# Cross-attention on one core: low parts, a score tile, bias additions and normalization moved within the slots

## The chip, the cores and the metric

The kernel runs on one core of a Trainium2 chip. The metric is the device time of the core in microseconds (us). Five engines work beside each other, each through its own list of instructions in the order in which the program wrote them: TensorE (PE; its weight loads are listed apart as PEld), VectorE (DVE), ScalarE (ACT), GpSimd (POOL) and SyncE (SP). SP computes nothing here. It issues nearly all DMAs, also in order, and an issue whose data is not ready holds up those behind it.

## The reference

Thirty-two batch entries share one set of weights. Each has 512 query rows of width 640 and 77 text keys of width 1024. Only the text part of the context is present (77 rows), so the three other attentions of the original network have no keys and add nothing.

```python
q   = heads(x @ to_q_w)                 # 32 x 20 heads x 512 x 32
k   = heads(ctx @ to_k_w)               # 32 x 20 heads x 77 x 32
v   = heads(ctx @ to_v_w)
p   = softmax(q @ k.T / sqrt(32))       # over the 77 keys
out = merge(p @ v) @ to_out_w + to_out_b + x
```

Everything is float32. The kernel gets products of that quality out of a faster, reduced format: each operand is split into a high part (a copy rounded to that format) and a low part (the operand less its high part), and each product is the sum of three: high by high, high by low, low by high.

## The kernel before

**Stages.** In the first part (the first score product starts at 262.2 us, and the last values follow beside the first slots) the keys and values of all batches are computed from the context, split into parts and written to scratch memory in HBM. After that comes attention, in *slots*. The width of 640 is cut into five chunks of 128, which are four heads each. Slot n = 5b + j works on batch b, chunk j, so a batch takes five slots and there are 160 of them. `end()` closes the pipeline behind the last.

**What one slot does.** `slot(n)` is the whole schedule: engines run their instructions in the order in which this function writes them, and nothing reorders them. The buffer counts (`bufs=`) set which earlier reader an instruction has to wait for. In one slot several chunks are in flight:

- `scores(n, t)`, t = 0 to 3: three score products (L478) of 128 query rows with the keys of four heads, into one of three PSUM tiles; VectorE takes the row maximum (L486). `exps(n, t)`: ScalarE's four exponentials with their sums (L496).
- `queries(n+1, ...)`: fifteen products (L443) for the next chunk's queries, then `split_q(n+1)`: ScalarE's high copy (L454), two GpSimd casts (L458) and two VectorE subtractions (L460). The next slot's scores need all of them.
- `sums(n-1)` takes the reciprocal of the sums (VectorE, L506), `normalize(n-1)` multiplies the probabilities of the last chunk by it (GpSimd, L511, one instruction of 16 rows of 77), and `transpose_p(n-1)` turns them in 32 by 32 blocks (VectorE, L518) and stores them to scratch memory (four DMAs, L525).
- `load_p(n-3)` fetches older probabilities back (L534, L535), now with keys along partitions. For the chunk `taken` = n-4, `cast_p` makes their high parts on ScalarE (L542 for the last 64 rows, L543 for the rest), `last_p` the low part of those 64 rows on GpSimd (L556) and `rest_p` that of the rest on VectorE (L549). All four write one buffer, `pp`.
- `values(taken)` is six value products (L570). The first two read L543's result; the third and fourth read rows written by L542 and L556 together; the fifth and sixth read L549's. They write `pa`, of which there is one. `sum_a` copies its upper half (ScalarE, L581) and adds it to the lower (VectorE, L583). In the next slot `high_a` and `low_a` split the sum (ScalarE L590, VectorE L595); this frees `pa`.
- `piece(batch, i)`: output products (L613), 24 per slot, of an earlier batch, in two pieces of 12 (6 and 18 in slot 4). `finish()` adds residual and bias to finished halves of an output tile (VectorE, L642) and sends the tile out (L648).

**Residual and bias.** An output tile has 128 rows; each batch has four, t = 0 to 3. `load_residual` (SP, L602) fetches rows of x into one of three buffers `xr`; `add_bias` (GpSimd, L606) adds the bias to them. Two tables say in which slot j of a batch b this happens, as (how many batches back, t): `RESIDUAL = {1: (1, 0), 3: (1, 1), 4: (1, 2), 0: (2, 3)}` and `BIAS = {2: (1, 0), 4: (1, 1), 0: (2, 2), 1: (2, 3)}`. So in a batch's slot 0, tile 3 of the batch before the last is fetched, and in slot 1 its bias is added. Tile 0 of the last batch is fetched in slot 1 and gets its bias in slot 2, where the first of its additions in `finish` is two slots away.

**Other work in the slots.** `split_x` (ScalarE L264, GpSimd L265) and `transpose_x` (VectorE L257) prepare the next batch's x; `copy_keys` (GpSimd, L423, L424) doubles some key rows, for one group of chunks in slot 1 and for the other in slot 4; `refill` and `load_x` fetch keys, values and x (L419, L432, L253).

**Orders that the change touches.** GpSimd's order in slot 1 is `copy_keys`, `last_p`, `normalize`, the two casts of `split_q`, `add_bias`; in slot 0 it is `last_p`, `normalize`, casts, `add_bias`. VectorE runs `rest_p` and then `low_a`, except in slot 4, where `low_a` is first. SP's order in slot 0 is: one fetch of x, four of keys, the two of `load_p`, four more of keys, the residual, and then the four stores of `transpose_p`.

## Time and profile before

| What | us |
|---|---|
| runs shown: median of 3 (lowest to highest) | 1933.45 (1927.69 to 1944.38) |
| the profiled execution: its own time | 1923.57 |
| its span, first to last instruction | 1921.7 |
| mean granted TensorE clock in it | 0.992 |
| GpSimd's bias additions, L606 | 128 of 1.584 each, 202.7 in all |
| GpSimd's normalization, L511 | 160 of 3.147 each, 503.5 in all |
| VectorE's low part of the probabilities, L549 | 160 of 1.632 each |
| VectorE's low part of attention, L595 | 160 of 0.680 each |

The profile is of one execution, which lies 0.5% under the median of the runs shown. Its times are from the start of the span. A row of a group gives the busy time, the mean of one instruction, and the idle time of the engine before these instructions with what ended it. Matmuls are pipelined and their ends are modelled, so TensorE's progress is better read from the starts of its instructions than from its busy time. In a timeline, a row can stand for several like instructions (x12), and the bracket at its end gives the idle time before it and the instruction or DMA that ended it.

### The profile page before, as it was taken

The page shows a single profiled execution, that of the slowest core. Times are in us where ns is not written, and L with a number is a line of the kernel's source. Part 1 is how long each engine was busy: PE and PEld are TensorE (multiplying, and loading weights), DVE is VectorE, ACT ScalarE, POOL GpSimd, SP SyncE. Part 2 cuts the span into 40 slices and gives each one's busy share as a digit, 9 for nine tenths or more (in the row PEclk, how much of TensorE's full clock was granted, in tenths as well). Part 3 has the DMA queues.
Part 4 walks back from the last instruction along what each step waited for, and adds up shares of the span by engine and source line. Part 5 has one row for each costly group of instructions (what it writes and reads, how often), then busy time and mean ns, then how long its engine had stood idle before and what let it go on. Part 6 is the DMA issues. An engine that isn't in the chain of part 4 may idle for free.

```text
span 1921.7 us, 37548 instructions
## 1 busy us (share of the span) xinstructions
PE 1883.1 (98%) x10332; PEld 1665.2 (87%) x10332; DVE 1626.7 (85%) x2494; ACT 1526.3 (79%) x6210; POOL 1422.3 (74%) x1116
## 2 busy tenths in 40 slices
PE   9999997999999999999999999999999999999998
PEld 7888886888888888888888889888888888888887
DVE  5444447899999989999999999999999999999985
ACT  3232247998998989899888899998998989999882
POOL 1100067888898888888888888888888888888873
PEclk9999998999999999999999999999999999999999
DMA  9878869898888888888989898898889888889875
GB/s 185 201 195 249 200 176 222 215 233 238 235 232 233 233 216 231 233 231 228 238 223 236 236 239 234 232 237 231 234 228 233 225 240 234 237 232 229 226 211 157
DMA packets 565022, 431.36 MB, mean 224 GB/s; under 512 B 191120, under 2 KB 473168, under 8 KB 564816
## 3 DMA queue, kind: packets, MB, share of 16 engines
q1 hardware_dynamic: 560304, 414.47, 84.0%
q0 software_dynamic: 4416, 14.34, 2.2%
q8 instruction: 85, 1.39, 0.3%
q14 instruction: 121, 0.99, 0.2%
q10 hardware_dynamic: 96, 0.16, 0.0%
HBM read 247.17 MB, written 181.64 MB: 223 GB/s over the span
## 4 chain that ended last, share of the span: by engine, by line
PE 44%; ACT 15%; DVE 14%; DMA 13%; issue 5%; SPq 5%; POOL 3%; DVEq 0%; POOLq 0%; ACTq 0%
PE pq L443 11%; PE po L613 11%; PE pv L191 6%; DMA raw<-pd 6%; ACT pn L496 6%; PE pk L191 6%; PE pa L570 5%; PE sc L478 4%; DVE pp L549 4%; DMA xs<-in_x_dram 3%; ACT pp L543 2%; DVE nm L486 2%; DVE z L518 2%; ACT xt L264 2%; ACT aw L581 2%
## 5 line engine op out<-in xcount | busy, mean ns | idle before, releaser
L496 ACT ACTIVATE pn<-sc,nm 128x77 f32<-128x77 f32 x2560 | 794.0, 333 | 32.6 <-DVE nm L486 27.7
L613 PE MATMUL po<-wo_s,at 128*128 128x320 f32 x3840 | 636.1, 314 | 7.3 <-DVE at L595 3.0
L443 PE MATMUL pq<-xt,wq_s 128*128 128x512 f32 x2400 | 621.4, 400 | 0.0
L613 PEld LDWEIGHTS po<-wo_s,at 128*128 128x128 f32 x3840 | 569.0, 189 | 15.9 <-DVE at L595 12.3
L496 ACT ACTIVATION_READ_ACCUMULATOR pn<-sc,nm 128x1 f32 x2560 | 545.7, 213 | 0.0
L511 POOL TENSOR_TENSOR pn<-pn,rs 128x1232 f32<-128x1232 f32 x160 | 503.5, 3147 | 23.8 <-DVE rs L506 12.3
L443 PEld LDWEIGHTS pq<-xt,wq_s 128*128 128x128 f32 x2400 | 429.9, 190 | 75.7
L478 PEld LDWEIGHTS sc<-kb,qt 128*128 128x128 f32 x1920 | 327.9, 189 | 59.7 <-POOL qt L458 12.1
L478 PE MATMUL sc<-kb,qt 128*128 128x154 f32 (+1 forms) x1920 | 317.9, 274 | 13.8 <-POOL qt L458 8.9
L486 DVE TENSOR_REDUCE nm<-sc 128x4 f32<-128x308 f32 x640 | 288.4, 451 | 44.1 <-PE sc L478 37.6
L549 DVE TENSOR_TENSOR pp<-raw,pp 128x1024 fp32r<-128x1024 f32 x160 | 261.1, 1632 | 31.0 <-ACT pp L543 24.9
L556 POOL TENSOR_TENSOR pp<-raw,pp 64x512 fp32r<-64x512 f32 x160 | 212.4, 1327 | 97.5 <-ACT pp L542 88.5
L570 PE MATMUL pa<-pp,vb 128*128 128x512 f32 x960 | 265.5, 407 | 10.0 <-DVE at L595 6.2
L518 DVE STREAM_TRANSPOSE z<-pn 128x1280 f32<-128x1280 f32 x160 | 241.9, 1512 | 8.0 <-DMA pd<-z 2.8
L583 DVE TENSOR_TENSOR pa<-pa,aw 64x512 f32<-64x512 f32 x320 | 222.7, 696 | 21.1 <-ACT aw L581 10.8
L460 DVE TENSOR_TENSOR qt<-pq,qt 64x512 fp32r<-64x512 f32 x320 | 219.2, 685 | 23.6 <-ACT qt L454 17.0
L265 POOL TENSOR_TENSOR xt<-xs,xt 128x512 fp32r<-128x512 f32 x160 | 202.6, 1292 | 34.0 <-ACT xt L264 30.7
L570 PEld LDWEIGHTS pa<-pp,vb 128*128 128x128 f32 x960 | 171.8, 190 | 57.8 <-DVE pp L549 13.2
L606 POOL TENSOR_TENSOR xr<-xr,bias 128x640 f32<-128x640 f32 x128 | 202.7, 1584 | 17.6 <-DMA xr<-in_x_dram 6.0
L458 POOL CAST qt<-qt 64x512 fp32r<-64x512 f32 x320 | 195.0, 609 | 21.7 <-ACT qt L454 2.0
L581 ACT COPY aw<-pa 64x1024 f32<-64x1024 f32 x160 | 161.9, 1012 | 47.5 <-PE pa L570 43.3
L542 ACT CAST pp<-raw 64x512 fp32r<-64x512 f32 x160 | 99.5, 622 | 97.6 <-DMA raw<-pd 97.3
(46 smaller groups left out, 1639.8 us busy)
## 6 DMA issues: line engine op xcount, KB each, us to landing
pd<-z SPq DMA_DIRECT2D x640, 160.0 KB, 3.5
raw<-pd SPq DMA_DIRECT2D x160, 512.0 KB, 4.0
xs<-in_x_dram SPq DMA_DIRECT2D x128, 320.0 KB, 7.2
xr<-in_x_dram SPq DMA_DIRECT2D x128, 320.0 KB, 3.8
out_dram<-xr SPq DMA_DIRECT2D x127, 320.0 KB, 3.7
raw<-pd SPq DMA_DIRECT2D x160, 128.0 KB, 4.2
v_dram<-vs SPq DMA_DIRECT2D x80, 192.0 KB, 4.1
k_dram<-ks POOLq DMA_DIRECT2D x20, 512.0 KB, 4.3
```

Source lines behind the costliest of these rows:

```text
L191: nc.tensor.matmul(held[j][:, :gn], w[:, k, a, :], cts[g, k][:, c, :gn], start=(k == 0 and n == 0), stop=(k == NK - 1 and n == 2),)
L443: nc.tensor.matmul(pqs[n], wq_s[:, k, a, j * P : (j + 1) * P], xts[b, k][:, c, :], start=(k == 0 and m == 0), stop=(k == NC_ - 1 and m == 2),)
L460: nc.vector.tensor_tensor(qt[r, 1 + w, :], pq[r], qt[r, 0, :].bitcast(F32), ALU.subtract)
L478: nc.tensor.matmul(sc[:, cols], qt[:, m, t * P : (t + 1) * P], keys_, start=(m == 0), stop=(m == 2),)
L486: nc.vector.tensor_reduce(nm, sc[:, :KCOLS].rearrange("p (h k) -> p h k", k=NKEY), AX.X, ALU.max, negate=True)
L496: nc.scalar.activation(pnb[n % 2][:, at, :NKEY], sc[:, i * NKEY : (i + 1) * NKEY], AF.Exp, bias=nm[:, i : i + 1], accum_out=sms[n][:, at : ...
L511: nc.gpsimd.tensor_tensor(pf, pf, rs.unsqueeze(2).to_broadcast([P, NQ * HPC, NKEY]), ALU.mult)
L518: nc.vector.transpose(z.rearrange("p b t j -> p t b j"), pn.rearrange("p (t h) k -> p t (h k)", t=NQ).rearrange("p t (b i) -> p t b i", i=Q),)
L549: nc.vector.tensor_tensor(pp[:, 2:4, :], raw[:, 0:2, :], pp[:, 0:2, :].bitcast(F32), ALU.subtract)
L570: nc.tensor.matmul(pas[n][:, p, :], vb[:, p, t, :], pp[:, c, :], start=(c == p), stop=(c == p + 2),)
L583: nc.vector.tensor_tensor(pa[64 * p : 64 * p + 64, 0], pa[:64, p], aw[:, p], ALU.add)
L613: nc.tensor.matmul(pos[b, t, h][:, :HALF], ats[b * NC_ + j][:, a, t * P : (t + 1) * P], wos[0][:, j, c, h * HALF : (h + 1) * HALF], start= ...
```

## The change

Seven things move; no arithmetic is added or left out.

1. `low_a` goes ahead of `rest_p` in slots 0 to 3. In slot 3, `high_a` also goes between the two casts of `cast_p`.
2. In slots 0 to 3, once output products run, the third score tile comes after four of the six value products instead of after all six.
3. The bias of tile 3 is added in slot 0 instead of slot 1, that of tile 0 in slot 1 instead of slot 2. The loads stay where they are.
4. `normalize` becomes two instructions of eight rows each. In slot 4 the second comes after the casts of `split_q`.
5. In slots 1 and 2 `normalize` goes ahead of `last_p`, and in slot 1 `copy_keys` goes from the slot's start to behind `last_p`.
6. In slots 4, 0 and 1 the reciprocal of the slot's own sums is taken at its end, ahead of the two additions of `sum_a`, instead of at the start of the next slot.
7. In slot 2 both splits of x come before the copy of `pa`, instead of one before and one after.

```diff
@@ -506,11 +506,13 @@
         nc.vector.reciprocal(rs, sms.pop(n))
         return rs
 
-    def normalize(n, rs):
-        pf = pnb[n % 2][:, :, :NKEY]
-        nc.gpsimd.tensor_tensor(
-            pf, pf, rs.unsqueeze(2).to_broadcast([P, NQ * HPC, NKEY]), ALU.mult
-        )
+    def normalize(n, rs, halves=(0, 1)):
+        half = NQ * HPC // 2
+        for k in (i * half for i in halves):
+            pf = pnb[n % 2][:, k : k + half, :NKEY]
+            nc.gpsimd.tensor_tensor(
+                pf, pf, rs[:, k : k + half].unsqueeze(2).to_broadcast([P, half, NKEY]), ALU.mult
+            )
 
     def transpose_p(n):
 
@@ -535,11 +537,13 @@
         nc.sync.dma_start(raw[:64, 2, :], pd[P : P + 64, :])
         raws[n] = raw
 
-    def cast_p(n):
+    def cast_p(n, between=None):
 
         raw = raws[n]
         pp = late[0].tile([P, 5, S], FPR, tag="pp", name="pp", bufs=1)
         nc.scalar.copy(pp[:64, 4, :], raw[:64, 2, :])
+        if between is not None:
+            between()
         nc.scalar.copy(pp[:, 0:2, :], raw[:, 0:2, :])
         pps[n] = pp
 
@@ -561,12 +565,13 @@
 
     PASSES = [(p, t, c + p * (t == 0)) for t, c in ((0, 0), (1, 4), (0, 2)) for p in range(2)]
 
-    def values(n):
+    def values(n, i0=0, i1=6):
         b, j = divmod(n, NC_)
         g = GROUP_OF[j]
-        pp, vb = pps.pop(n), vbs[g][:, j - GROUPS[g][0]]
-        pas[n] = late[1].tile([P, 2, S], F32, tag="pa", name="pa", bufs=1)
-        for p, t, c in PASSES:
+        pp, vb = pps[n], vbs[g][:, j - GROUPS[g][0]]
+        if i0 == 0:
+            pas[n] = late[1].tile([P, 2, S], F32, tag="pa", name="pa", bufs=1)
+        for p, t, c in PASSES[i0:i1]:
             nc.tensor.matmul(
                 pas[n][:, p, :],
                 vb[:, p, t, :],
@@ -575,12 +580,18 @@
                 stop=(c == p + 2),
             )
 
-    def sum_a(n):
-        pa = pas[n]
-        aw = late[0].tile([64, 2, S], F32, tag="aw", name="aw", bufs=1)
-        nc.scalar.copy(aw, pa[64:])
+    def copy_a(n):
+        aws[n] = late[0].tile([64, 2, S], F32, tag="aw", name="aw", bufs=1)
+        nc.scalar.copy(aws[n], pas[n][64:])
+
+    def add_a(n):
+        pa, aw = pas[n], aws.pop(n)
         for p in range(2):
             nc.vector.tensor_tensor(pa[64 * p : 64 * p + 64, 0], pa[:64, p], aw[:, p], ALU.add)
+
+    def sum_a(n):
+        copy_a(n)
+        add_a(n)
 
     def high_a(n):
         if n >= N - NC_ + 1:
@@ -656,9 +667,9 @@
 
     PIECES = {3: (1, 0), 4: (1, 2), 0: (2, 4), 1: (2, 6), 2: (2, 8)}
     RESIDUAL = {1: (1, 0), 3: (1, 1), 4: (1, 2), 0: (2, 3)}
-    BIAS = {2: (1, 0), 4: (1, 1), 0: (2, 2), 1: (2, 3)}
+    BIAS = {4: ((1, 1),), 0: ((2, 2), (2, 3)), 1: ((1, 0),)}
     TRANSPOSE_X = {0: ((), (), (0,)), 1: ((1,), (), (2,)), 2: ((3,), (), ())}
-    SPLIT_X = {2: ((0,), (1,)), 3: ((2, 3), (4,))}
+    SPLIT_X = {2: ((0, 1), ()), 3: ((2, 3), (4,))}
 
     WO = {1: (0, 1, 2), 2: (3, 4)}
     wos = []
@@ -697,37 +708,50 @@
         if not filling:
             refill(b, j, 0)
         copied = {1: 1, 4: 0 if more else None}.get(j)
-        if has_out and copied is not None:
+        if has_out and copied == 0:
             copy_keys(copied)
-        if taken is not None and j != NC_ - 1:
+            copied = None
+
+        def high():
+            if n - 1 in takes:
+                high_a(takes[n - 1])
+
+        if taken is not None and j < 4:
+            cast_p(taken, high if has_out and j == 3 else None)
+        if not (has_out and j == 3):
+            high()
+        if taken is not None and j == 4:
             cast_p(taken)
-        if n - 1 in takes:
-            high_a(takes[n - 1])
-        if taken is not None and j == NC_ - 1:
-            cast_p(taken)
-        bias_now = j in BIAS and b >= BIAS[j][0]
-        if bias_now and not ahead:
-            add_bias(b - BIAS[j][0], BIAS[j][1])
+        biases = [(b - back, t) for back, t in BIAS.get(j, ()) if b >= back]
+        if not ahead:
+            for bias_of in biases:
+                add_bias(*bias_of)
         s = scores(n, 0)
         if j == 2:
             finish()
-        rs = sums(n - 1) if n else None
+        if n and n - 1 not in rss:
+            rss[n - 1] = sums(n - 1)
+        if has_out and j in (1, 2):
+            normalize(n - 1, rss.pop(n - 1))
         if taken is not None:
             last_p(taken)
-        if not has_out and copied is not None:
+        if copied is not None:
             copy_keys(copied)
-        if n:
-            normalize(n - 1, rs)
+        parted = j == 4 and has_out and ahead
+        if n - 1 in rss:
+            normalize(n - 1, rss[n - 1], (0,) if parted else (0, 1))
+            if not parted:
+                rss.pop(n - 1)
         exps(n, 0, *s)
         if ahead:
             queries(n + 1, 0, 2)
         if j == NC_ - 1 and n - 1 in takes:
             low_a(takes[n - 1])
         s = scores(n, 1)
+        if j != NC_ - 1 and n - 1 in takes:
+            low_a(takes[n - 1])
         if taken is not None:
             rest_p(taken)
-        if j != NC_ - 1 and n - 1 in takes:
-            low_a(takes[n - 1])
         if n == LATE:
             nc.sync.dma_start(bias, bo.unsqueeze(0).to_broadcast([P, C]))
         if n >= LATE:
@@ -764,8 +788,10 @@
             transpose_p(n - 1)
         if ahead:
             split_q(n + 1)
-            if bias_now:
-                add_bias(b - BIAS[j][0], BIAS[j][1])
+            if parted:
+                normalize(n - 1, rss.pop(n - 1), (1,))
+            for bias_of in biases:
+                add_bias(*bias_of)
             exps(n, 2, *s)
         if j == 4 and b + 2 < B:
             load_x(b + 2, (2,))
@@ -786,20 +812,26 @@
             if n:
                 transpose_p(n - 1)
         if taken is not None and not (early and j == 4):
-            values(taken)
+            values(taken, 0, 4 if has_out else 6)
         if len(beside) > 0:
             context_values(LAST, beside[0], psv)
         if has_out:
             s = scores(n, 3)
+            if j != 4:
+                values(taken, 4, 6)
             transpose_p(n - 1)
         finish()
         for i in turns[1]:
             transpose_x(b + 1, i)
         if taken is not None:
-            sum_a(taken)
+            copy_a(taken)
         for c in xsplits[1]:
             split_x(b + 1, c)
         exps(n, 3, *s)
+        if has_out and j in (4, 0, 1):
+            rss[n] = sums(n)
+        if taken is not None:
+            add_a(taken)
         if len(beside) > 1:
             context_values(LAST, beside[1], psv)
         if has_out:
```

More of the change, by code (lines that the diff above doesn't have):

```diff
@@ L391 @@
     late = []
-    raws, pps, ats, pds, sms, pqs, pas, xrs, pos = ({} for _ in range(9))
+    raws, pps, ats, pds, sms, pqs, pas, xrs, pos, aws, rss = ({} for _ in range(11))
     bias = main.tile([P, C], F32, name="bias")
```

## The prediction

> **What bounds the kernel now.** I read the page's busy times first, then the busy times of the stretch from 400 to 1800 us, where the slots repeat, then the waits, then one batch line by line. The page's first line, and the answer for that stretch (columns: its length, then busy us and instructions of each engine, granted clock, DMA share, GB/s):
>
> ```profile
> PE 1883.1 (98%) x10332; PEld 1665.2 (87%) x10332; DVE 1626.7 (85%) x2494; ACT 1526.3 (79%) x6210; POOL 1422.3 (74%) x1116
> ...
> 400.00:1800.00 1400.00, 1390.85 (x7934) 1240.97 (x7933) 1308.34 (x2003) 1260.43 (x5289) 1202.83 (x919) 1.00 0.89 232
> ```
>
> TensorE is the bound, at full clock, with VectorE 93%, ScalarE 90% and GpSimd 86% busy behind it: whatever is moved lands in a queue with little room. From the waits (total us, times, longest us):
>
> ```profile
> PEld pa L570 <- DVE pp L549: 13.2, 29, 0.6
> PEld po L613 <- DVE at L595: 12.3, 29, 1.4
> PEld pa L570 <- DVE at L595: 10.2, 26, 1.8
> ```
>
> Three waits, each about once per batch of five slots: 35.7 us in all. The first score products of batches 2 and 31 start at 365.62 and 1824.85 us, so a batch takes 1459.2/29 = 50.3 us. A slot without a wait, slot 0 of batch 16, runs from 1072.57 to 1082.39, 9.8 us; five make 49.1. So 1.2 us per batch, 36 us in 30 batches, is all that any reordering can win here: the floor is 1923.6 - 36 = 1888 us.
>
> Now slots 0 and 1 of batch 16, on GpSimd, then on SP's queue, then on TensorE (start, duration, instruction; in brackets the idle time before it):
>
> ```profile
> 1079.14 1.27 POOL L458 CAST qt<-qt 64x512 fp32r<-64x512 f32 x2
> 1080.50 1.57 POOL L606 TENSOR_TENSOR xr<-xr,bias 128x640 f32<-128x640 f32 x1
> 1082.74 0.43 POOL L423 CAST kb<-kb 64x308 fp32r<-64x308 f32 x1 [0.67 <-DMA kb<-k_dram]
> 1085.28 0.44 POOL L424 CAST kb<-kb 64x308 fp32r<-64x308 f32 x1 [2.12 <-DMA kb<-k_dram]
> 1085.81 1.28 POOL L556 TENSOR_TENSOR pp<-raw,pp 64x512 fp32r<-64x512 f32 x1
> 1087.17 3.14 POOL L511 TENSOR_TENSOR pn<-pn,rs 128x1232 f32<-128x1232 f32 x1
> 1090.37 1.27 POOL L458 CAST qt<-qt 64x512 fp32r<-64x512 f32 x2
> 1091.73 1.57 POOL L606 TENSOR_TENSOR xr<-xr,bias 128x640 f32<-128x640 f32 x1
> ```
>
> ```profile
> 1073.52 2.89 SPq L525 DMA_DIRECT2D pd<-z  x4
> ...
> 1083.43 0.42 SPq L602 DMA_DIRECT2D xr<-in_x_dram  x1
> ```
>
> ```profile
> 1086.90 1.96 PE L613 MATMUL po<-wo_s,at 128*128 128x320 f32 x12
> 1088.83 1.67 PE L570 MATMUL pa<-pp,vb 128*128 128x512 f32 x6
> 1092.46 0.50 PE L478 MATMUL sc<-kb,qt 128*128 128x308 f32 x3
> ```
>
> The reader should see three things. GpSimd's last part of the probabilities (L556) ends at 1087.09, and the third value product, which reads it, is due at 1089.17 (output products from 1086.90 for 12 x 0.15, then two value products of 0.235): 2.1 us to spare. The residual tile that SP fetches at 1083.43 is used only by the bias at 1091.73. And SP reaches that fetch late because its queue, idle since 1070.99, waits for the transpose of slot 4 (ended 1073.49) and then runs without a pause.
>
> **The change part by part.**
>
> *Attention's low part first.* L595 moves ahead of L549 in slots 0 to 3, and in slot 3 its high copy moves between the two casts. It then starts about 1.6 us sooner (L549's mean, 1632 ns), more than either of its two waits (12.3/29 = 0.4 us, 10.2/26 = 0.4): both go. L549 comes 0.7 us later (L595's 680 ns), but its reader is now behind four value products and a score tile (4 x 0.235 + 0.33 = 1.3 us): no cost. Without that cover it would add 0.7 us per slot.
>
> *Score tile after four value products.* Nothing is added on TensorE; the score tile is 0.47 us sooner, and the copy of pa on ScalarE (L581) is 0.33 us later. The page shows ScalarE already waiting there in 36 slots (43.3 us): between 0 and 0.33 us in one slot of a batch, hidden by the wait for raw after it. I take 0. The same holds of the x split that moves ahead of that copy in slot 2 (631 ns): L583, which reads the copy, is queued behind the transpose until after it.
>
> *Slot 4* keeps its order of products, so its wait for L549 (13.2/29 = 0.45) stays unless ScalarE, whose casts L549 waits for, starts earlier. What slot 3 wins is then waited for here; this wait is late next. Alone, these parts are worth between 0.3 and 1.2 us per batch.
>
> *Normalization in halves.* 160 more GpSimd instructions. By the rows, 640 elements take 1584 ns and 512 take 1292, so 616 cost about 1.5 to 1.6 us and a pair 3.1 to 3.3 against 3147 ns: 0 to 0.15 us per slot, hidden wherever GpSimd idles. In slot 4 the second half comes after the query casts, so the transpose starts later: averaged over 24 batches of the trace, ScalarE has the query 47.3 us into the batch, the casts take 1.35 and the half 1.6, which makes 50.3, where it now starts at 49.7: 0.6 us. SP's chain starts with that transpose, so I bound this at -1.3 (engines behind TensorE catch up in a longer batch) to +0.6 and take 0.
>
> *Reciprocal at the slot's end (slots 4, 0, 1).* Same instruction, 233 ns, now ahead of the two additions L583 and waiting for the last exponentials. In slot 0 VectorE reaches it around 1083.2 and ScalarE's last exponential ends about then: 0 to 0.7 us for L583, whose reader (L590) comes after two casts of 1.7 us. 0.
>
> *Bias a slot sooner, and the order on GpSimd.* This decides. The diff leaves the residual loads where they are. So the bias of tile 3 is now added in the slot that fetches it (slot 0), and that of tile 0 likewise (slot 1). In slot 0 GpSimd finishes the other bias at 1082.07 and then waits: the fetch is issued at 1083.43, after the fifteen issues that follow the transpose, and the DMA row says
>
> ```profile
> xr<-in_x_dram SPq DMA_DIRECT2D x128, 320.0 KB, 3.8
> ```
>
> so it lands at 1087.2. Behind that wait stand, in program order, the normalization of slot 1 (moved ahead of L556), L556, the key copies (first read in slot 3) and the query casts. The bias ends at 1088.8, the two halves at 1092.05, L556 at 1093.4, handoffs of 0.08 included. TensorE wants L556's result at 1089.17: **a new wait of 4.3 us in slot 1 of every batch**, against 2.1 us to spare now. The trace's shortest residual fetch, 2.8 us, makes it 3.3; with the bounds on SP's start it is 2.0 to 4.9. The query casts, after key copies of 0.9, end at 1095.8; TensorE, delayed to 1096.6 at the next slot's first scores, is not held again. Tile 0's fetch, now at 1093.16, lands about 1097, when GpSimd reaches it at about 1095.8: 1.2 us more on GpSimd, which slot 2 has back through one bias less (1.57).
>
> *The clock.* The profile shows what TensorE's idling does:
>
> ```profile
> 1866.97 0.56 PE L613 MATMUL po<-wo_s,at 128*128 128x320 f32 x2 [1.36 <-ACT at L590]
> ...
> 1868.43 2.93 PE L570 MATMUL pa<-pp,vb 128*128 128x512 f32 x6
> ```
>
> ```profile
> 1868.30:1871.70 3.40, 3.40 (x11) 2.65 (x10) 2.70 (x4) 3.40 (x24) 3.32 (x2) 0.50 1.01 249
> ```
>
> After an idle 1.36 us the clock stood at 0.50 for 3.4 us, and six value products took 2.93 us instead of 1.57; at 786 us an idle 1.49 changed nothing. An idle 4.3 us is well beyond both. One such stretch of 3.4 us at roughly half rate (267 ns between output products against 147) loses 1.5 us; two would lose 3.1, none 0. I take 1.5, the only duration seen after one single gap.
>
> The Trainium skill's "TensorE: Matmul & The Clock Gate" (HAM oscillation — how this bites in real kernels) sets the limit at idle gaps over about 3.4 us and bills a case of such gaps 1.67 us throttled each, half of it lost. The row above is stricter, since 1.36 us sufficed. By the page the clock would cost an estimated 0.84 us per batch, 25 us in all, where the row gives 46; and it would cost nothing if the wait came out at 3.3 us.
>
> The skill's "DMA: Bandwidth & Descriptors" (Rules for kernel authors) speaks against this edit: issue the DMA early and wait late. No run here prices that.
>
> **Sum.** In a longer batch the other engines catch up and the old waits go: 49.1 + 4.3 + 1.5 = 54.9 us against 50.3, so +4.6. Batches 2 to 31 have both slots: 30 x 4.6 = 138. The profiled execution took 1923.57 us (span 1921.7), which is 0.5% under the median of 1933.45. 1923.6 + 138 = 2062; a third of the 10 us offset on top gives **2065 us**.
>
> **Rivals.**
>
> *The stall without the clock.* 49.1 + 4.3 - 50.3 = 3.1 us; x30 = 93: 2017 us, or 1987 with the shortest fetch (2.1 x 30 = 63). For: 1.49 us without effect at 786 us. Against: the row at 1868 us.
>
> *A longer stall.* 4.9 us and two slow stretches: 49.1 + 4.9 + 3.1 - 50.3 = 6.8; x30 = 204: 2128 us. For: the slot 4 half delays SP's chain.
>
> *Faster.* GpSimd's idle 2.8 us before the key copies really is filled and the three waits go: 1888 to 1910 us. It decides if the tile lands by 1083.0, because 1083.0 + 1.57 + 3.2 + 1.29 + handoffs is 1089.2; that is before its fetch is even issued now. SP would have to be 4.2 us earlier in its queue, and nothing in the diff shortens it.
>
> *It does little*: part of the wait is absorbed, the old waits' 1.2 us repay the rest: 1915 to 1960.
>
> **How the numbers follow.** Stall with one slow stretch 0.5, stall without 0.2, longer stall 0.15, little 0.08, faster 0.07. Faster by over 1% is the faster case, 0.07; within 1%, which is about what a measurement of this kernel can tell from no change, 0.05 from the little case; the rest, 0.88, slower. The range leaves out the faster and the little case below and the far end of the longer stall above: 1987 to 2130.
>
> **What would show it.** Right: GpSimd's L606 waiting for the DMA of xr some 30 times, about 5 us each; TensorE's pa waiting for POOL pp (L556 before, renumbered) some 30 times, about 4 us; the waits for L595 gone; mean clock near 0.97 (half rate in 3.4 of every 55 us). Wrong: that L606 wait short, or TensorE's 2.1 us to spare in slot 1 still there.

## The result, and the profile after

The changed kernel takes 2068.52 us (median of 4, 2064.43 to 2069.32) against 1938.37 us before (median of 4, 1927.69 to 1944.38): a ratio of 1.067, 95% interval 1.064 to 1.069, so 130 us more. The profiled execution took 2064.43 us, 141 us more than the one of before. Of all executions told of below one stands out, 4608.12 us of c1_whole4; no trace shows why, and its ratio goes by the other nine. Line numbers move: the bias L606 is now L617, the last low part L556 is L560, the value products L570 are L575, the rest's low part L549 is L553, the normalization L511 is L513, attention's low part L595 is L606, the output products L613 are L624 and the residual fetch L602 is L613.

From the page of the changed kernel, the busy time of each engine:

```profile
PE 1919.6 (93%) x10332; PEld 1704.8 (83%) x10332; DVE 1660.0 (80%) x2494; ACT 1537.9 (75%) x6210; POOL 1392.8 (68%) x1276
```

and its busy times from 400 to 1800 us (columns as before: length, busy us and instructions of PE, PEld, DVE, ACT and POOL, granted clock, DMA share, GB/s):

```profile
400.00:1800.00 1400.00, 1303.13 (x7253) 1170.32 (x7252) 1227.57 (x1832) 1163.91 (x4838) 1074.41 (x969) 0.96 0.84 212
```

The work is the same (10332 matmuls), yet every engine, TensorE too, is busy for a smaller share, and the clock fell from 1.00 to 0.96. No engine has become the bound: something holds them all up together. The waits of the changed kernel (total us, times, longest us) name it:

```profile
POOL xr L617 <- DMA xr<-in_x_dram: 152.7, 45, 6.2
...
PE pa L575 <- POOL pp L560: 114.0, 34, 5.0
...
DVE z L520 <- POOL pn L513: 26.2, 34, 2.3
...
PE pa L575 <- DVE at L606: 3.7, 4, 1.9
...
PEld po L624 <- DVE at L606: 0.9, 2, 0.4
```

GpSimd waits for the residual tile, once or twice per batch, and TensorE waits for GpSimd, about once. The weight loads' waits for attention's low part (L606), 22.5 us before, are down to 0.9; on the matmuls' own row 3.7 us are left. One batch whose scores start at 971.98 us shows the order. First GpSimd in slots 0 and 1:

```profile
978.37 1.28 POOL L458 CAST qt<-qt 64x512 fp32r<-64x512 f32 x2 [1.43 <-ACT qt L454]
979.73 1.57 POOL L617 TENSOR_TENSOR xr<-xr,bias 128x640 f32<-128x640 f32 x1
986.01 1.57 POOL L617 TENSOR_TENSOR xr<-xr,bias 128x640 f32<-128x640 f32 x1 [4.71 <-DMA xr<-in_x_dram]
987.53 3.38 POOL L513 TENSOR_TENSOR pn<-pn,rs 128x616 f32<-128x616 f32 x2
990.99 1.26 POOL L560 TENSOR_TENSOR pp<-raw,pp 64x512 fp32r<-64x512 f32 x1
...
995.35 1.56 POOL L617 TENSOR_TENSOR xr<-xr,bias 128x640 f32<-128x640 f32 x1 [0.76 <-DMA xr<-in_x_dram]
```

Then SP's queue, where the fetch of that tile (L613) is issued at 982.51, behind the stores of slot 4 and eleven more fetches:

```profile
973.11 2.37 SPq L527 DMA_DIRECT2D pd<-z  x4
...
982.51 0.43 SPq L613 DMA_DIRECT2D xr<-in_x_dram  x1
```

Then TensorE, where the third value product waits for L560, and the twelve output products after it take 3.31 us where the twelve before took 1.96:

```profile
986.35 1.96 PE L624 MATMUL po<-wo_s,at 128*128 128x320 f32 x12
988.15 0.63 PE L575 MATMUL pa<-pp,vb 128*128 128x512 f32 x2
992.30 0.73 PE L575 MATMUL pa<-pp,vb 128*128 128x512 f32 x2 [3.52 <-POOL pp L560]
...
993.86 3.31 PE L624 MATMUL po<-wo_s,at 128*128 128x320 f32 x12
```

The stretch behind that wait, with columns as in the row from 400 to 1800 us, has the clock at 0.50:

```profile
993.50:996.90 3.40, 3.40 (x14) 3.31 (x13) 2.21 (x4) 2.73 (x10) 2.58 (x4) 0.50 0.43 124
```

### The profile page after: what moved, and what is told of

It is laid out like the page before. It is cut to its first block, busy times and chain, and to the rows that moved or that the text cites. A ratio compares the mean times of both kernels' runs of the same rounds, so it can differ in the third digit from the quotient of the medians.

```text
span 2062.7 us, 37659 instructions
## 1 busy us (share of the span) xinstructions
PE 1919.6 (93%) x10332; PEld 1704.8 (83%) x10332; DVE 1660.0 (80%) x2494; ACT 1537.9 (75%) x6210; POOL 1392.8 (68%) x1276
## 4 chain that ended last, share of the span: by engine, by line
PE 30%; issue 16%; DVE 13%; DMA 12%; ACT 11%; POOL 11%; SPq 6%; POOLq 0%; DVEq 0%; ACTq 0%
PE po L624 11%; PE pq L443 10%; POOL pn L513 6%; PE pa L575 5%; ACT pn L496 5%; PE sc L478 4%; DMA raw<-pd 3%; DVE pp L553 3%; DMA xs<-in_x_dram 3%; POOL pp L560 3%; DMA xr<-in_x_dram 2%; DVE z L520 2%; DMA pd<-z 2%; SPq L419 2%; DVE pa L590 2%
## 5 line engine op out<-in xcount | busy, mean ns | idle before, releaser
L624 PE MATMUL po<-wo_s,at 128*128 128x320 f32 x3840 | 650.2, 321 | 1.5 <-ACT at L601 1.2
L624 PEld LDWEIGHTS po<-wo_s,at 128*128 128x128 f32 x3840 | 604.9, 197 | 15.6 <-ACT at L601 1.6
L513 POOL TENSOR_TENSOR pn<-pn,rs 128x616 f32<-128x616 f32 x320 | 479.9, 1517 | 26.3 <-DVE rs L506 11.0
L575 PE MATMUL pa<-pp,vb 128*128 128x512 f32 x960 | 304.0, 426 | 119.9 <-POOL pp L560 114.0
L478 PEld LDWEIGHTS sc<-kb,qt 128*128 128x128 f32 x1920 | 335.1, 194 | 63.3 <-POOL qt L458 12.0
L478 PE MATMUL sc<-kb,qt 128*128 128x154 f32 (+1 forms) x1920 | 323.5, 277 | 15.0 <-POOL qt L458 7.5
L617 POOL TENSOR_TENSOR xr<-xr,bias 128x640 f32<-128x640 f32 x128 | 204.7, 1600 | 180.3 <-DMA xr<-in_x_dram 152.7
L553 DVE TENSOR_TENSOR pp<-raw,pp 128x1024 fp32r<-128x1024 f32 x160 | 287.2, 1795 | 22.0 <-ACT pp L547 17.8
L575 PEld LDWEIGHTS pa<-pp,vb 128*128 128x128 f32 x960 | 168.6, 198 | 155.2 <-POOL pp L560 130.5
L560 POOL TENSOR_TENSOR pp<-raw,pp 64x512 fp32r<-64x512 f32 x160 | 209.1, 1307 | 57.8 <-ACT pp L544 40.3
L547 ACT CAST pp<-raw 128x1024 fp32r<-128x1024 f32 x160 | 168.5, 1053 | 0.0
```

Source lines behind the costliest of these rows:

```text
L478: nc.tensor.matmul(sc[:, cols], qt[:, m, t * P : (t + 1) * P], keys_, start=(m == 0), stop=(m == 2),)
L513: nc.gpsimd.tensor_tensor(pf, pf, rs[:, k : k + half].unsqueeze(2).to_broadcast([P, half, NKEY]), ALU.mult)
L553: nc.vector.tensor_tensor(pp[:, 2:4, :], raw[:, 0:2, :], pp[:, 0:2, :].bitcast(F32), ALU.subtract)
L560: nc.gpsimd.tensor_tensor(pp[64:, 4, :], raw[:64, 2, :], pp[:64, 4, :].bitcast(F32), ALU.subtract)
L575: nc.tensor.matmul(pas[n][:, p, :], vb[:, p, t, :], pp[:, c, :], start=(c == p), stop=(c == p + 2),)
L624: nc.tensor.matmul(pos[b, t, h][:, :HALF], ats[b * NC_ + j][:, a, t * P : (t + 1) * P], wos[0][:, j, c, h * HALF : (h + 1) * HALF], start= ...
```

## All runs in one table

A slot is read from the start of its first score product to that of the next slot, as a mean over batches 6 to 29 of the profiled execution. The last column is the time that TensorE spent below full clock in the whole execution. The floor of a slot, its mean where TensorE does not wait, is 9.82 us.

| Kernel | median us | ratio to before (95%) | slots 0, 1, 2, 3, 4 (us) | batch | low clock |
|---|---|---|---|---|---|
| before | 1938.37 | 1 | 9.84 10.04 10.06 10.23 10.15 | 50.32 | 31.6 |
| changed | 2068.52 | 1.067 (1.064 to 1.069) | 9.84 15.41 9.95 9.85 9.99 | 55.04 | 142.7 |
| a1_bias_back | 1953.21 | 1.012 (1.010 to 1.013) | 9.83 10.07 9.92 10.06 11.37 | 51.25 | 30.2 |
| b1_bias_only | 1992.76 | 1.031 (1.028 to 1.033) | 9.96 12.63 10.18 9.86 9.92 | 52.55 | 77.8 |
| a3_last_first | 1985.51 | 1.028 (1.026 to 1.029) | 9.84 11.21 11.18 9.86 9.99 | 52.09 | 40.2 |
| a2_warm | 2042.31 | 1.057 (1.056 to 1.059) | 9.82 14.05 9.87 9.85 10.67 | 54.26 | 29.8 |
| c4_fetch_first | 2069.77 | 1.074 (1.068 to 1.079) | 9.85 9.93 15.30 9.87 9.90 | 54.84 | 136.7 |
| d1_fetch_and_bias | 1971.20 | 1.022 (1.017 to 1.027) | 9.83 10.08 10.19 10.26 11.42 | 51.77 | 25.1 |
| d3_together | 1961.75 | 1.016 (1.013 to 1.020) | 9.83 10.12 10.13 10.02 11.41 | 51.51 | 28.1 |
| c2_low_only | 2021.17 | 1.047 (1.043 to 1.051) | 9.84 10.53 11.37 10.85 11.09 | 53.68 | 14.9 |
| c3_low_score | 2030.06 | 1.051 (1.046 to 1.056) | 9.83 10.39 11.13 10.81 11.44 | 53.60 | 21.9 |
| d2_low_short_norm | 1929.14 | 0.999 (0.997 to 1.002) | 9.85 9.87 9.93 9.90 11.00 | 50.55 | 17.2 |
| c1_whole4 | 1943.25 | 1.006 (1.004 to 1.008) | 9.83 9.85 9.87 10.27 11.30 | 51.13 | 27.8 |
| e1_large_first | 1948.19 | 1.008 (1.006 to 1.010) | 9.84 9.91 9.92 9.98 11.42 | 51.07 | 24.7 |

Each kernel is compared with runs of the kernel before beside it, so the ratio, not the difference to 1938.37, is what to read. The profiled execution of before (1923.57 us) is shorter than its four runs, and that of c1_whole4 (1949.75) is the longest of its nine, so slots of these two kernels differ by more than their medians do.

## Is it the bias? Undone, and done alone

The change with the old table of biases:

```diff
-    BIAS = {4: ((1, 1),), 0: ((2, 2), (2, 3)), 1: ((1, 0),)}
+    BIAS = {2: ((1, 0),), 4: ((1, 1),), 0: ((2, 2),), 1: ((2, 3),)}
```

> The changed kernel with the bias additions in their old slots; all else as changed. Theory (GpSimd waits for the residual tile fetched in the same slot, and the part of the probabilities that TensorE needs is queued behind that wait): the 3.7 us wait of TensorE in slot 1 goes, and with it the slow clock: 2068 - 30 x (3.7 + 1.7) = 1906 us, 1890 to 1930, clock 0.99, no GpSimd wait for xr. Rival (the order of GpSimd in slots 1 and 2, the halves or VectorE's new wait cost as much): stays above 1960.

Slot 1 fell from 15.41 to 10.07 us, and the low clock to 30.2 us, what it was before the change. Of GpSimd's waits for the tile one is left, at the end of the execution (1926 us). It and two others in the waits of that kernel (total, times, longest):

```profile
POOL xr L617 <- DMA xr<-in_x_dram: 6.4, 1, 6.4
...
DVE z L520 <- POOL pn L513: 23.1, 32, 0.8
...
PEld pa L575 <- DVE pp L553: 28.2, 42, 0.8
```

So the bias is the cause of nearly all of the loss. But the rest of the change, of which the theory expected a gain (1890 to 1930 us), costs 1.2% by itself, so the time is in neither range. It shows in slot 4 (11.37 against 10.15): 23.1/32 = 0.7 us in which VectorE's transpose waits for the second half of the normalization, and TensorE's wait for L553.

The kernel before with the new table alone (and the loop that reads it):

```diff
-    BIAS = {2: (1, 0), 4: (1, 1), 0: (2, 2), 1: (2, 3)}
+    BIAS = {4: ((1, 1),), 0: ((2, 2), (2, 3)), 1: ((1, 0),)}
```

> The kernel before with the bias additions moved as in the change, and nothing else. Theory: GpSimd gets the residual tile at 14.1 us into the batch and ends its bias at 15.7; then key copies, L556 of the kernel before (ends about 18.0, due at 16.6: TensorE waits 1.4 us), normalization and the query casts (end about 22.6, due at 21.1: another 1.5 us). 30 x 2.9 = 87 us more than 1938, 2025, and up to 2065 if the clock drops too. Rival (it takes the new order on GpSimd to lose anything, the bias alone is hidden): within 1% of 1938.

```profile
POOL xr L606 <- DMA xr<-in_x_dram: 158.5, 36, 6.3
...
PE pa L570 <- POOL pp L556: 54.5, 31, 2.4
```

These are waits of that kernel. GpSimd waits as long as in the full change (158.5 us), but TensorE waits 1.7 us per batch instead of 3.7, because here the last low part still goes ahead of the normalization. The expected second wait, 1.5 us at the scores of slot 2, hardly came (slot 2 takes 10.18 us), so the loss is 60 us where 87 or more were expected. The table alone costs 3.1%, the rest alone 1.2%, together they cost 6.7%: the two are not a sum. The changed order in slot 1 explains the surplus, as the next run shows.

The change with the last low part ahead of the normalization again in slots 1 and 2:

```diff
-        if has_out and j in (1, 2):
-            normalize(n - 1, rss.pop(n - 1))
         if taken is not None:
             last_p(taken)
+        if has_out and j in (1, 2):
+            normalize(n - 1, rss.pop(n - 1))
```

> The changed kernel with L560 (last part of the probabilities) ahead of the normalization again in slots 1 and 2; the bias waits as in the change. Theory: GpSimd's bias ends at 15.9, L560 at 17.2, due at 16.6: TensorE's wait for it falls from 3.7 to 0.6 us; but normalization, key copies and query casts then end about 22.8, due at 20.3: a wait of 2.5 us at the next slot's scores takes its place. Total wait 3.1: 2068 - 30 x 0.6 = 2050, 2030 to 2060 with what the clock does. Rival (the place of L560 behind the normalization is the whole loss): 1930 to 1960.

```profile
PE pa L575 <- POOL pp L560: 34.9, 33, 2.5
...
PE sc L478 <- POOL qt L458: 29.4, 59, 2.5
```

This one edit takes 83 us off the changed kernel (77 by the ratios); the time lies between the two expectations. TensorE's wait in slot 1 is 1.02 us instead of 3.72, too short for the clock to fall in most batches (40.2 us of low clock). A smaller part, 0.86 us, comes back at the scores of slot 2, which wait for the query casts: GpSimd's delay still has to end somewhere. The fetch makes the delay, and the 3.3 us of normalization between it and L560 decide who feels it.

## What the clock costs

The change with fourteen more value products ahead of the wait in slot 1, whose result is overwritten; they keep TensorE at work through the wait:

```diff
+            values(taken, 0, 2)
+            held = ps.tile([P, S], F32, tag="sc", name="sc", bufs=3)
+            for _ in range(14):
+                nc.tensor.matmul(held, vb[:, 0, 0, :], pps[taken][:, 0, :], start=True, stop=True)
+            values(taken, 2, 4)
```

> The changed kernel with 14 extra value products in slot 1 of each batch, between the second and the third, into a score tile that the scores overwrite afterwards: about 3.3 us of TensorE work inside the wait of 3.7 us; the output does not use them. Theory (the wait is set by GpSimd's chain, and the slow clock after it is a second cost of about 1.7 us per batch): clock back to 0.985 or more, time down by 30 x 1.7 = 51, to about 2017 us, though more work is done. Rival (the clock costs nothing because the next limit hides it, or TensorE's work is what counts): same as 2068, or 30 x 3.3 = 99 us more, 2167.

```profile
POOL xr L618 <- DMA xr<-in_x_dram: 141.2, 43, 6.9
...
PE pa L576 <- POOL pp L561: 20.3, 30, 2.1
...
PE pa L576 <- DVE pp L554: 10.2, 29, 0.4
```

GpSimd still waits, TensorE's clock is full from 355 to 2010 us, and slot 1 is 1.36 us shorter (14.05), although its third value product starts 0.15 us later (10.88 us into the slot for 10.73). From that start to the slot's end it takes 3.17 us instead of 4.68, so the clock costs 1.51 us; 3.31 - 1.96 = 1.35 of that is in the twelve output products shown above. But the batch is only 0.78 us shorter, and the kernel won 26 us (20 by the ratios) of the expected 51, because slot 4 grew by 0.68: the wait for the low part (L554) is back there. That the other engines have less time to catch up at full clock would explain it; no run tests that.

## Can the fetch be made early enough?

The change with tile 3 fetched first in SP's queue of slot 0, ahead of the keys:

```diff
-    RESIDUAL = {1: (1, 0), 3: (1, 1), 4: (1, 2), 0: (2, 3)}
+    RESIDUAL = {1: (1, 0), 3: (1, 1), 4: (1, 2)}
...
+            if not part and b >= 2:
+                load_residual(b - 2, 3)
             load_keys(b, 1, heads)
```

> The changed kernel with one DMA moved: the residual of tile 3 is issued on SP's queue in slot 0 ahead of the key loads (after 5 issues instead of 15 behind the transpose). Theory: it lands about 9.0 us into the batch instead of 14.1, GpSimd goes from one bias to the next without a wait, normalization and L560 of slot 1 end near 15.5, before they are due at 16.6; TensorE's wait goes, clock 0.99: near the run with the old bias slots, 1953, 1940 to 1970, which still has the wait in slot 4. Rival (two biases and the normalization ahead of L560 are too much for GpSimd even with the tile there): 1990 or more.

The time is in the rival's range, but not for its reason. The tile lands 10.0 us into the batch (mean) instead of 14.1, and TensorE's wait in slot 1 is gone; it turns up in slot 2. GpSimd in that kernel, in slots 0 to 2 of a batch that starts at about 975 us:

```profile
986.17 1.56 POOL L617 TENSOR_TENSOR xr<-xr,bias 128x640 f32<-128x640 f32 x1 [1.81 <-DMA xr<-in_x_dram]
...
990.18 1.28 POOL L560 TENSOR_TENSOR pp<-raw,pp 64x512 fp32r<-64x512 f32 x1
...
999.93 1.57 POOL L617 TENSOR_TENSOR xr<-xr,bias 128x640 f32<-128x640 f32 x1 [4.83 <-DMA xr<-in_x_dram]
1001.47 3.38 POOL L513 TENSOR_TENSOR pn<-pn,rs 128x616 f32<-128x616 f32 x2
1004.92 1.26 POOL L560 TENSOR_TENSOR pp<-raw,pp 64x512 fp32r<-64x512 f32 x1
```

Slot 1 is cured (9.93 us), and slot 2 now has the whole loss (15.30): tile 0 is also fetched in the slot that uses it. In the changed kernel that second wait was 0.8 us, because the first had already made GpSimd late. A wait can cover another of the same kind behind it.

So both were taken away, with tile 3 fetched first and tile 0's bias back in slot 2:

```diff
-    BIAS = {4: ((1, 1),), 0: ((2, 2), (2, 3)), 1: ((1, 0),)}
+    BIAS = {4: ((1, 1),), 0: ((2, 2), (2, 3)), 2: ((1, 0),)}
```

> The run with the earlier fetch of tile 3, and the bias of tile 0 back in slot 2, a slot after its own fetch. Theory (with tile 3 there in time, the wait of GpSimd had only moved to the second bias that stands in the slot of its fetch, tile 0 in slot 1, and TensorE's wait with it to slot 2): both waits go, slots 1 and 2 take 10.0 us each instead of 9.9 and 15.3, clock 0.99, 1940 to 1960. Rival (something else in slot 2 holds GpSimd): 2000 or more.

```profile
POOL xr L617 <- DMA xr<-in_x_dram: 25.8, 26, 6.1
...
PE pa L575 <- POOL pp L560: 1.5, 1, 1.5
```

TensorE's waits are gone, and GpSimd's for the tile are down to some 0.8 us each; yet the kernel is still 2.2% slower than before, 11 us above the upper end of what was expected. What remains is the rest of the change.

## What the rest of the change costs: the low part that goes first

The kernel before with only the first item of the change, attention's low part ahead of the probabilities':

```diff
-        if taken is not None:
-            rest_p(taken)
         if j != NC_ - 1 and n - 1 in takes:
             low_a(takes[n - 1])
+        if taken is not None:
+            rest_p(taken)
```

(with the high copy between the casts in slot 3, as in the change).

> The kernel before with attention's low part ahead of L549 in slots 0 to 3 and the high copy between the casts in slot 3, and nothing else. Theory (ScalarE's chain from slot 3 to slot 4 sets when L549 of slot 4 can run, so what slot 3 wins is waited for in slot 4): the waits for L595 in slots 1 to 3 go, the wait in slot 4 grows from 0.3 to about 0.9 us, time within 10 us of 1932. Rival (the won time stays): 0.7 us per batch, 21 us, about 1911.

Both theories missed: it is 4.7% slower. The waits of that kernel show on what:

```profile
PE pa L572 <- DVE pp L551: 83.6, 99, 2.0
```

TensorE now waits for the very instruction that was to be delayed at no cost. It is not only later, it is longer; in the groups of that kernel (after the bar: busy us, mean ns of one, then idle time):

```profile
L551 DVE TENSOR_TENSOR pp<-raw,pp 128x1024 fp32r<-128x1024 f32 x160 | 397.9, 2487 | 22.0 <-ACT pp L545 17.8 <-DMA pd<-z 0.3
```

2487 ns for what took 1632 before. The timelines show it beside GpSimd's normalization, before the change:

```profile
1075.68 3.40 POOL L511 TENSOR_TENSOR pn<-pn,rs 128x1232 f32<-128x1232 f32 x1
...
1075.74 1.20 DVE L549 TENSOR_TENSOR pp<-raw,pp 128x1024 fp32r<-128x1024 f32 x1
```

and in c2_low_only:

```profile
1016.04 2.28 POOL L511 TENSOR_TENSOR pn<-pn,rs 128x1232 f32<-128x1232 f32 x1 [0.19 <-DVE rs L506]
...
1016.74 2.65 DVE L551 TENSOR_TENSOR pp<-raw,pp 128x1024 fp32r<-128x1024 f32 x1
```

Starting nearly together, VectorE takes 1.20 us and GpSimd's 2.28 becomes 3.40. Starting 0.70 us after GpSimd, VectorE takes 2.65 and GpSimd keeps its 2.28. The rule can be read off all 160 instructions of each trace: for VectorE's low part, which GpSimd instruction was running when it started, and how long both took (means). Small groups, and slots in which GpSimd ran nothing then, are left out.

| Kernel | GpSimd's instruction | slots | it started ahead by | its time | VectorE's time | VectorE's time less what was left of it |
|---|---|---|---|---|---|---|
| before | normalization | 43 | 0.11 us | 3.45 | 1.20 | VectorE ends first |
| before | normalization | 1 | 0.66 | 2.27 | 2.69 | 1.08 |
| before | last low part | 101 | 0.50 | 1.29 | 1.87 | 1.08 |
| c2_low_only | normalization | 7 | 0.09 | 3.45 | 1.22 | VectorE ends first |
| c2_low_only | normalization | 106 | 0.51 | 2.28 | 2.85 | 1.08 |
| c2_low_only | last low part | 39 | 0.38 | 1.29 | 1.99 | 1.08 |
| changed | a half of the normalization | 65 | 0.36 | 1.23 | 1.95 | 1.08 |
| changed | last low part | 38 | 0.40 | 1.29 | 1.97 | 1.08 |
| changed | bias | 29 | 0.85 | 1.57 | 1.80 | 1.08 |

When nothing ran on GpSimd it took 1.20. When something did, it either went first, or took what was left of that instruction plus 1.08 us, whatever the instruction (where under 0.12 us was left, 1.20 in all). So it isn't slowed; but for some 0.1 us it stands still until GpSimd's instruction ends, and then runs. The other way round, GpSimd stands still: 3.45 is 2.28 and 1.17. Before the change, VectorE reached the low part just in time to go first in 43 of the 44 slots in which it met the normalization. The 0.7 us of attention's low part ahead of it is enough to lose that race in nearly all of them.

The Trainium skill's "SBUF — State Buffer" (Who interferes with whom) says that a VectorE instruction with two inputs in SBUF contends with a GpSimd instruction that reads SBUF, and that the one that issues second blocks until the other is done. The table agrees. By the page alone, an estimate for 1016.74 would be 1.58 left of L511 and then 1.20: 2.78, where 2.65 was measured.

To test it, the same kernel with a normalization that does one of its 16 rows, so that the probabilities are left unscaled in the other 15:

```diff
-        pf = pnb[n % 2][:, :, :NKEY]
+        pf = pnb[n % 2][:, :1, :NKEY]
```

> The run with attention's low part first alone (2021 us), with the normalization cut to one of its 16 rows, so the output is not normalized: work is left out of GpSimd, about 2.8 us per slot, nothing is left out of VectorE. Theory (L551, which takes 2.66 us in slots 0 to 3 instead of 1.2 to 1.9, is longer because it now starts after the normalization and runs beside it): L551 falls to 1.2 to 1.4 us in slots 0 to 2, TensorE's waits for it there go, 1900 to 1930. Rival (the low part's place itself, or ScalarE's copies, make L551 long): it stays at 2.4 us or more and the time above 1980.

```profile
L551 DVE TENSOR_TENSOR pp<-raw,pp 128x1024 fp32r<-128x1024 f32 x160 | 225.8, 1411 | 25.1 <-ACT pp L545 17.9 <-DMA pd<-z 6.4
```

The mean falls from 2487 to 1411 ns and all 92 us of the loss are gone: slots 0 to 3 stand at 9.85 to 9.93 us. So the normalization's presence is the cost; that it is the collision follows from the table, since this run also frees GpSimd of 1.9 us per slot (2561 to 690 ns) and can't separate the two. And the low part first does win in these four slots when nothing is in its way, 40.17 - 39.55 = 0.62 us per batch. Slot 4, at 11.00 against 10.15, takes it all back.

The score tile amid the value products, added to c2_low_only:

```diff
-            values(taken)
+            values(taken, 0, 4 if has_out else 6)
...
             s = scores(n, 3)
+            if j != 4:
+                values(taken, 4, 6)
```

> The same and the third score tile after four of six value products in slots 0 to 3. The prediction put these two parts together at 0.3 to 1.2 us per batch: 1932 - 9 to 36, 1896 to 1923. Theory as for the low part alone: VectorE gets the score 0.47 us sooner, but ScalarE's copy of pa comes 0.33 later, slot 4 still waits for ScalarE's casts: 1915 to 1935. Rival: 1905 or less, the waits are gone.

This is far above both expectations, and the intervals overlap with those of c2_low_only (1.043 to 1.051, and 1.046 to 1.056). TensorE's wait in slots 1 to 3 shrinks from 2.46 to 1.88 us per batch, since the last two value products come 0.33 us later, but the batch is only 0.08 us shorter. The score tile's effect can't be told from none.

## What slot 4 takes back

Without the bias, and with the normalization in one piece in slot 4 (from a1_bias_back):

```diff
-        parted = j == 4 and has_out and ahead
+        parted = False
```

> The run with the old bias slots (1953 us), and in slot 4 the normalization as two halves one after the other in the old place, instead of the second behind the query casts. Theory (the second half makes VectorE's transpose of slot 4 wait 0.75 us for GpSimd; the additions, high copy and exponentials behind it start later, ScalarE's casts in slot 4 end later by as much, and TensorE waits there): that wait of VectorE goes, slot 4 falls from 11.4 to about 10.4 us, 1953 - 30 = 1923, 1915 to 1940. Rival (VectorE's L553, which is longer beside the earlier normalization, 9.0 against 8.2 us per batch, holds slot 4): 1945 or more.

The second half behind the casts had cost 10 us (1953.21 to 1943.25; the four runs of a1_bias_back and the nine that count here do not overlap). VectorE's wait for it, 23.1 us before, is gone, but slot 4 stands at 11.30 us and not at the expected 10.4, and neither range holds the time:

```profile
DVE z L520 <- POOL pn L513: 0.5, 2, 0.2
...
PEld pa L575 <- DVE pp L553: 32.3, 47, 0.8
```

The largest wait left in slot 4 is that for L553, which there starts behind the last low part on GpSimd and takes 2.12 us. So its two casts on ScalarE were exchanged, to let VectorE go first:

```diff
+        if large_first:
+            nc.scalar.copy(pp[:, 0:2, :], raw[:, 0:2, :])
         nc.scalar.copy(pp[:64, 4, :], raw[:64, 2, :])
...
-        nc.scalar.copy(pp[:, 0:2, :], raw[:, 0:2, :])
+        if not large_first:
+            nc.scalar.copy(pp[:, 0:2, :], raw[:, 0:2, :])
```

> The run with the old bias slots and the whole normalization in slot 4 (1943 us; slots 0 to 2 without a wait, slot 3 at 10.3, slot 4 at 11.3 us), with ScalarE's two casts of slot 4 in the other order: L553's input first, L560's second. Theory (slot 4 is held by L553, which waits for the second of the two casts and then runs beside L560): L553 starts 0.63 us sooner and ahead of L560, so it takes 1.2 to 1.6 us instead of 2.1 and ends 1.1 to 1.5 us sooner; L560 ends 1.1 us later, about when it is due; slot 4 near 10.1, 1943 - 33 = 1910, 1900 to 1922. Rival (the fetch of the probabilities sets ScalarE's chain, or the query products' wait for GpSimd's x split in slot 4 is next): 1930 or more.

Slot 4 of one batch of that kernel (TensorE, VectorE, GpSimd; its L578, L556 and L563 are L575, L553 and L560 of the changed kernel):

```profile
1080.75 1.20 PE L578 MATMUL pa<-pp,vb 128*128 128x512 f32 x4 [0.92 <-POOL pp L563]
...
1078.35 1.22 DVE L556 TENSOR_TENSOR pp<-raw,pp 128x1024 fp32r<-128x1024 f32 x1
...
1078.86 1.84 POOL L563 TENSOR_TENSOR pp<-raw,pp 64x512 fp32r<-64x512 f32 x1 [0.38 <-ACT pp L546]
```

VectorE's part fell to 1.22 us as expected, and GpSimd's rose to 1.84, since it now has to stand still. TensorE, which needs both, waits for the other one. The time did not fall; it is in the rival's range.

Last, several edits in one kernel: d1_fetch_and_bias with the whole normalization in slot 4, the normalization first in slots 0 to 2, and the fetches of `load_p` ahead of the value fetches in slot 2:

```diff
+        loads_first = has_out and j == 2
+        if loads_first:
+            load_p(n - LAG + 1)
...
-        if has_out and j in (1, 2):
+        if has_out and j in (0, 1, 2):
...
-        parted = j == 4 and has_out and ahead
+        parted = False
```

> The run just named (tile 3 fetched first, tile 0's bias in slot 2), with the normalization whole in slot 4, ahead of L560 in slots 0, 1 and 2, and in slot 2 the fetch of the probabilities ahead of the values on SP's queue. Theory: slots 0 to 2 at 9.85 us; slots 3 and 4 still wait for ScalarE's casts and L553, 0.4 us less than in the run with the whole normalization (1943): 1925 to 1943. Rival (slots 3 and 4 are freed too): below 1915.

It won 0.5% over d1_fetch_and_bias, and at 1962 us is above both expectations and still 1.6% behind the kernel before. No version beat that one. Three versions bring slots 0 to 3 near their floor (39.6 to 39.8 us together, against 40.17), and in each of them slot 4 is 11.0 to 11.4 us. What holds slot 4 can be read in c1_whole4 (GpSimd, VectorE, TensorE):

```profile
972.87 3.79 POOL L265 TENSOR_TENSOR xt<-xs,xt 128x512 fp32r<-128x512 f32 x3 [0.37 <-PE sc L478]
...
977.88 1.29 POOL L560 TENSOR_TENSOR pp<-raw,pp 64x512 fp32r<-64x512 f32 x1
...
978.13 2.12 DVE L553 TENSOR_TENSOR pp<-raw,pp 128x1024 fp32r<-128x1024 f32 x1 [0.37 <-ACT pp L547]
...
976.71 0.73 PE L443 MATMUL pq<-xt,wq_s 128*128 128x512 f32 x2 [0.29 <-POOL xt L265]
...
980.30 0.73 PE L575 MATMUL pa<-pp,vb 128*128 128x512 f32 x2 [0.35 <-DVE pp L553]
```

From the three splits of x on, GpSimd runs into the next batch without a pause. The query products that read the last part of x start 0.06 us after its split ends, the third value product 0.05 us after L560, and the fifth 0.05 us after L553, which stood still behind L560 (means over batches 6 to 29). By the starts of TensorE's instructions these three delays cost 0.5, 0.3 and 0.6 us, together nearly all of the 1.5 us by which slot 4 exceeds the floor; the idle times of the profile show less than half of it. So slot 4 is held by GpSimd's queue, which is 0.8 us later there than before the change (L560 of slot 4 ends 46.4 us into the batch for 45.6). Which of GpSimd's earlier waits makes it late no run shows.

## Why the prediction was right, and where it was not

**The wait.** The chain was the one predicted, step by step (us from the batch's start, mean over batches; in brackets the prediction's times less 1072.57): fetch issued at 10.71 (10.9), landed at 14.13 (14.6), bias ended 15.87 (16.2), normalization 19.18 (19.5), L560 20.51 (20.8), query casts 22.85 (23.2). TensorE was idle for 3.72 us, and its third value product started 3.88 us later than in c4_fetch_first, whose slot 1 has no such wait (10.73 and 6.85 us into the slot), for 4.3 predicted. The term was 0.4 too large, most of it the fetch's transit, 3.42 us where the DMA row's median of 3.8 was taken.

**The clock.** One stretch of 3.4 us at half rate per batch was predicted, at 1.5 us. It is (142.7 - 31.6)/30 = 3.7 us of low clock per batch: 24 of 30 batches have it, nine of them for twice as long. It costs 1.5 to 1.6 us directly (4.68 us from the third value product to the end of slot 1, against 3.17 in a2_warm and 3.08 in c4_fetch_first), and 0.78 net. In b1_bias_only waits of 1.7 us, none above 2.4 on TensorE's own row, raised the low clock from 31.6 to 77.8 us, as the stricter row of before had it. The limit of some 3.4 us in the Trainium skill's "TensorE: Matmul & The Clock Gate" (HAM oscillation — how this bites in real kernels) doesn't show here: a wait of 3.72 at the mean lies above it, and those 2.4 us lie below it and still lowered the clock. Its estimate of 0.84 us is near the net cost, but a2_warm shows that to be the direct cost less what slot 4 gives back.

**The sum.** With slot 1 as in c4_fetch_first (9.93 us) the five slots would take 49.56 us, and 49.56 + 3.88 + 1.60 = 55.04, what the batch took; 49.1 + 4.3 + 1.5 = 54.9 was predicted. So the total owes some of its closeness to errors of opposite sign: a wait 0.4 too large, a floor not quite reached. 4.72 x 30 = 142 against the 138 predicted.

**Tile 0's fetch** cost GpSimd 0.76 us in the batch shown, for 1.2 predicted, and was harmless. It was harmless only behind the longer wait: alone, in c4_fetch_first, it cost as much as tile 3's.

**Slot 4.** The transpose that SP's chain waits for ended 1.35 us into the next batch instead of 0.92, inside the bounds of -1.3 to +0.6 for which 0 was taken. That slot 4 would be the next to wait was right. In the changed kernel, as in the others in which GpSimd's wait for a tile lengthens slot 1 or 2, slot 4 takes 9.9 to 10.0 us (10.67 in a2_warm); in the five that keep the rest of the change without that loss it is the longest slot (11.3 to 11.4).

**The step that failed** is "L549 comes 0.7 us later ... no cost", and with it "alone, these parts are worth between 0.3 and 1.2 us per batch". Its duration was taken from the group's mean, 1632 ns, as a property of the instruction. That mean is made of 1.20 us where it goes ahead of the normalization and 1.87 us where it finds the last low part running; moved by 0.7 us its mean became 2.49. The prediction put the edit without its cover of four value products and a score tile at 0.7 us per slot, and the cover at 1.3 us. Alone (c2_low_only), the edit costs 3.36 us per batch (53.68 - 50.32); with the cover (c3_low_score) it still costs 3.28 instead of winning. In the full change the halves, and the normalization moved ahead in slots 1 and 2, take the edge off (1795 ns), and the long slot 1 hides what is left. That is why the forecast survived it.

**The halves** were put at 3.1 to 3.3 us a pair whatever the place. The rows show 3.38 in one slot and, in c4_fetch_first at 987.69, 2.41 in another. Beside the 3.38 of the batch shown VectorE ran its low part, from 987.19 to 988.66, and by the table GpSimd stands still for some 1.1 us of it.

## What to carry to other kernels

Before moving a use of fetched data a step earlier, look where in its queue the fetch is issued: a wait on an engine that works in order is paid by everything behind it, and what stands between the wait and the instruction that the bound engine needs adds to the price (here 3.3 us of normalization). And when a group's mean hides a spread (1.20 to 2.69 us here for one shape), find out on what it depends before moving anything by some tenths of a us; on two engines that block each other, the order of their starts is part of the schedule. A gain in some stages counts only when the stage that closes the loop has room for it.

## What the hardware showed that was not expected

VectorE's two-input subtraction of 128 x 1024 in SBUF and GpSimd's instructions exclude each other almost completely: 1.20 us when alone or first, what is left of GpSimd's instruction plus 1.08 us when second, within 0.015 us in 378 of 383 such cases of three traces (those with more than 0.12 us left). Which of the two goes first can't be read from the recorded starts alone: VectorE went first in 57 cases although GpSimd was recorded to start up to 0.41 us earlier, and in others GpSimd went first with a lead of 0.01 us. What decides there stays open.

A gap on TensorE of 1.7 us on average halved the clock for 3.4 us in 11 of 30 batches (b1_bias_only); gaps of 3.6 us on average did so in 24 of 30 (changed). The length alone doesn't decide: in the changed kernel a gap of 2.61 us was followed by the low clock, one of 3.39 was not. The granted clock shows what does. In all 14 traces it changes only at instants that lie whole multiples of 3.413 us apart. Of the steps between two such instants at full clock, all 110 in which the matmul row was busy for under 46% were followed by a step at half clock, none of the 7696 above 63%, and 23 of the 135 between. So what counts is how much of a gap falls into one step.
